# Layer 1 of a two-layer graph network: first row factors moved by 256 bytes, and a group's end turned one row tile at a time

## Chip, cores and metric

The kernel runs on one core of one Trainium2 chip. The metric is the device time of one launch in microseconds (us). Three runs of the kernel before took 2812.17, 2810.19 and 2810.7 us; their median, 2810.7 us, is what the changed kernel is held against.

## The reference, cut to what matters

Two layers over 4096 nodes with 512 features, each with a LayerNorm and a ReLU ahead of it and a residual behind it. The change touches layer 1 only, which is an attention over all nodes with 8 heads of 64 columns:

```
data1 = (h @ W.T + b).reshape(N, H, D)
src = einsum('nhd,xhd->nh', data1, src_proj); trg = einsum('nhd,xhd->nh', data1, trg_proj)
e = src.T[:, :, None] + trg.T[:, None, :]
e = where(e >= 0, e, 0.01 * e) + adj
out = einsum('hnm,hmd->hnd', softmax(e), data1)
x = x + out
```

The kernel writes exp(leaky(src + trg) + adj) as a product of a row factor (z, one per head and destination node), column factors (g_m and d_m, one per head and source node) and exp(adj). So a tile of the scores is one `max` and one multiplication by exp(adj).

## The kernel before, in words

**Groups and steps.** Layer 1 runs over 8 groups: 4 blocks of 1024 destination nodes (WL) times 2 sets of 4 heads (HG). A group has 32 steps (NT), one for each tile of 128 source nodes, m = 0 to 31. In every step VectorE (DVE) makes the score tiles `pr` of the four heads (L1168 and L1171, 128x1024 each; in every fourth step, `BY_LOG`, ScalarE makes that of head 0), and TensorE (PE) multiplies them with the values (`values`, L1205) and with a column of factors for the softmax's denominators (`den`, L1210).

**How TensorE is filled.** The value matmuls have 32 columns of weights each, so four of them stand side by side in the array, in column groups 0 to 3 of 32 columns. `cols` in `gather` is the order in which a step addresses the four. A step gives each column group five matmuls: four of L1205 and one of L1210. In the seven steps of `BY_HALF` (4, 8, 12, 16, 20, 24, 28) one more matmul is given to one column group, number n, and the order turns by one afterwards: n is 0, 1, 2, 3, 0, 1, 2 in these seven steps. The last step gives nine more, to the column groups 0, 1, 2, 3, 1, 2, 3 and, at its end, 0 and 1.

**The end of a group.** ScalarE (ACT) copies the four results out of PSUM (`os`, and `od` for the denominators), and the rest is done during the next group, by `finish`: in its step 1 eight small matmuls sort the denominators (L1262), in step 2 VectorE takes their reciprocals (L1266). Then eight row tiles of 128 nodes are to be turned: `turn` (L1278) transposes two 128x128 pieces for each, on the whole array, into `pt`; ScalarE scales them (L1307, four activations for a tile) into `o`; a GpSimd DMA adds the residual x1 to `o` (taken from the list `due` in every fourth step); a SyncE DMA stores `o`. `finish` is a generator that is advanced in the steps listed in `PARTS`: row tiles are turned in pairs, one pair in each of the steps 2, 6, 10 and 14, after that step's matmuls, and the two tiles of a pair are scaled in the two parts that follow. The last group has its own ending, `finish_last`, which is not changed.

**The order of the work.** All of it is written out by hand (`manual_schedule`): each engine's queue holds its instructions in the order of the program. The loop at the end goes through `stages` (load 4 steps ahead, exp(adj) 1 ahead, weighing 1 ahead, ScalarE's factors 2 ahead, and so on, `gather` last) and then advances the ending.

**The start of layer 1.** The loads of the first row factors z (L1364, four DMAs on SyncE's queue, head 3 first) stand behind the load of the first adjacency tile. They need memory. The tiles of layer 1 lie in memory that layer 0 gave back; the pools `mid` and `l1` begin at the same address. Behind that address, per partition, `mid` takes 5,248 bytes, and he_t[0], he_t[1] and he_t[2] take 8,192 each, so he_t[2] ends at 29,824. In layer 1 the l1 tiles take 4,384, six `pr` tiles 24,576, and the pool s0 608 (pick 32, gap 64, zt0 512), so that z of head 3 begins at 29,568: 256 bytes within he_t[2]. That one holds the layer's bias and projection rows (L862) until the last product at L889. Then come `row_factors` (L1373 on VectorE, L1374 on ScalarE), the column factors g_m and d_m, the first step's four products, and `ngd_m` (L1394), which ScalarE's first `relus` (L1140) needs.

Of the kernel before, what the change touches and what calls it, by code (L numbers as in the profile page):

```python
# [8 lines left out]
FP = mybir.dt.float32  # L9
AF = mybir.ActivationFunctionType  # L10
ALU = mybir.AluOpType
# [4 lines left out]
P = 128  # L16
# [12 lines left out]
def kernel(  # L29
# [15 lines left out]
    nc = tc.nc  # L45
    N, F = x.shape
    H, D = 8, 64
    HG, WL = 4, 1024
    WT = WL // P
    NT = N // P  # L50
# [12 lines left out]
    x1 = dram.tile([N, F], FP, name="x1")  # L63
# [39 lines left out]
    with tc.tile_pool(name="w0", bufs=1) as wp, tc.tile_pool(name="a0", bufs=2) as ap_, tc.tile_pool(  # L103
        name="a0s", bufs=8
# [75 lines left out]
        def turn(t):  # L180
            b, j = divmod(t, TB)
            if j == 0:
                hts[b] = ap_.tile([P, KC, BL], FP, name="h_t")
            if t >= T0:
                nc.vector.transpose(
                    hts[b][:, :, j * P:(j + 1) * P].rearrange("p k (a q) -> p k a q", q=S),
                    hqs.pop(t).rearrange("p (a k q) -> p k a q", k=KC, q=S))
                return
            h = hs.pop(t)
            pt = pp.tile([P, KC, P], FP, name="bank")  # L190
            for k in range(KC):
                nc.tensor.transpose(pt[:, k, :], h[:, k * P:(k + 1) * P], ident)
            nc.vector.tensor_copy(hts[b][:, :, j * P:(j + 1) * P], pt)
            logit(t, h)
# [291 lines left out]
    with tc.tile_pool(name="mx0", bufs=1) as mx0, tc.tile_pool(name="b_b", bufs=3) as adj0, tc.tile_pool(  # L486
        name="mx1", bufs=1
    ) as mx1, tc.tile_pool(name="b_a", bufs=3) as adj1, tc.tile_pool(name="b_m", bufs=4) as mkp, tc.tile_pool(name="b_s", bufs=2) as sp, tc.tile_pool(
        name="b_p", bufs=6, space=PSUM
# [94 lines left out]
        for n in range(-5, len(items)):  # L584
# [3 lines left out]
            if n >= 0:  # L588
                i, j, t = items[n]
# [10 lines left out]
                if n in more:  # L600
                    f, m = more[n]
# [7 lines left out]
    with tc.tile_pool(name="c_x", bufs=1) as ldx, tc.tile_pool(name="c_y", bufs=1) as ldy, tc.tile_pool(  # L609
        name="c_d", bufs=2  # L610
    ) as wkp, tc.tile_pool(name="c_m", bufs=1) as mxp, tc.tile_pool(name="c_o", bufs=4) as iop, tc.tile_pool(
        name="c_s", bufs=2
    ) as sp, tc.tile_pool(name="c_q", bufs=1, space=PSUM) as p_q, tc.tile_pool(
        name="c_p", bufs=1, space=PSUM
# [12 lines left out]
        steps = [(n, q) for n in range(NB) for q in mixed(n)]  # L627
# [121 lines left out]
        left, scale, norms, zs = [], {}, iter(()), {}  # L749
# [25 lines left out]
        def denominators(n):  # L775
            b = ORDER_B[n]
            sc = sp.tile([P, TB], FP, name="sc")
            nc.vector.tensor_tensor(sc, zs.pop(n), dr[:, b * TB:(b + 1) * TB], ALU.add)
            nc.vector.reciprocal(sc, sc)
            nc.vector.tensor_tensor(sc, sc, na[:, b * TB:(b + 1) * TB], ALU.mult)  # L780
            scale[n] = sc
# [3 lines left out]
        def finish(n, j):  # L785

            b = ORDER_B[n]
            oc = iop.tile([P, F], FP, name="xt")
            blk[n][1].append(oc)
            for c, half in enumerate((2, 3) if j < 2 else (4, 5)):  # L790
                nc.scalar.activation(oc[:, c * F2:(c + 1) * F2], cs_[half][:, (j % 2) * F2:(j % 2 + 1) * F2], AF.Copy,
                                     scale=scale[n][:, j:j + 1])
            nc.gpsimd.dma_start(oc, xb_d[rows_of(b * TB + j), :], accum_op=ALU.add)
# [168 lines left out]
        pt = bank(7)  # L962
# [17 lines left out]
    g_m = l1.tile([P, H, NT], FP, name="g_m")  # L980
    d_m = l1.tile([P, H, NT], FP, name="d_m")
    ngd_m = l1.tile([P, H // HG, NT], FP, name="ngd_m")
# [27 lines left out]

    PARTS = (0, 1, 2, 4, 5, 6, 8, 9, 10, 12, 13, 14, 16, 17, 18, 22)
    BY_LOG = (3, 7, 11, 15, 19, 23, 27, 31)
    BY_HALF = (4, 8, 12, 16, 20, 24, 28)
    BY_DMA = [m for m in range(NT - 1) if m not in BY_HALF]
# [2 lines left out]
    with tc.tile_pool(name="p", bufs=2) as prp, tc.tile_pool(name="s0", bufs=1) as s0, tc.tile_pool(  # L1019
        name="za", bufs=1  # L1020
    ) as zp0, tc.tile_pool(name="e", bufs=4) as ep, tc.tile_pool(name="p0", bufs=3) as pr0p, tc.tile_pool(name="rl", bufs=2) as rlp, tc.tile_pool(
        name="io1", bufs=2
    ) as iop, tc.tile_pool(name="s1", bufs=1) as sp, tc.tile_pool(name="e3", bufs=2) as e3p, tc.tile_pool(
        name="zb", bufs=1
    ) as zp1, tc.tile_pool(name="ac", bufs=2) as acp, tc.tile_pool(
        name="os", bufs=1
    ) as osp, tc.tile_pool(name="u", bufs=1) as usp, tc.tile_pool(
        name="p_x", bufs=1, space=PSUM
# [35 lines left out]


        pick = s0.tile([P, 2, 4], FP, name="pick")
        s0.tile([P, 16], FP, name="gap")
        row = ident.rearrange("p (r s) -> p s r", s=Q)
        nc.vector.tensor_copy(pick, row[:, 0:2, :])
        nc.vector.tensor_tensor(pick[:, 1, 0:HV], pick[:, 1, 0:HV], row[:, 2, HV:2 * HV], ALU.add)  # L1070
# [52 lines left out]
        def early_logs(i, m):  # L1123
            logs(i, m, True)
# [15 lines left out]
            nc.scalar.activation(r, zs_[i, 0], AF.Relu, bias=ngd_m[:, h // HG, m:m + 1], scale=d_m[:, h, m:m + 1])  # L1140
            rl[i, m] = r

        due = []

        def sums(i, m):
            if m < 2:
# [5 lines left out]
        def weigh(i, m, order=ORDER):  # L1152
            if m % 4 == 1 and due:
                due.pop()()
            if m:
                sums(i, m - 1)
            h = groups[i][1] * HG
            x_ = ex.pop((i, m))
            for k in order:
                if (i, m, k) in pr:  # L1160
                    continue
                w = (prp if k else pr0p).tile([P, WL], FP, name=f"pr{k}")
                if k == 0 and (i, m) == (0, 0):
                    r = rlp.tile([P, WL], FP, name="rl")
                    nc.vector.tensor_scalar(r, zs_[0, 0], g_m[:, 0, 0:1], d_m[:, 0, 0:1], ALU.max, ALU.mult)
                    nc.vector.tensor_tensor(w, r, x_, ALU.mult)
                elif k == 0:
                    nc.vector.scalar_tensor_tensor(w, rl.pop((i, m)), ngd_m[:, h // HG, m:m + 1], x_,  # L1168
                                                   op0=ALU.subtract, op1=ALU.mult)
                else:  # L1170
                    p_ = nc.vector.scalar_tensor_tensor(w, zs_[i, k], g_m[:, h + k, m:m + 1],  # L1171
                                                        e3.pop((i, m)) if k == 3 else x_,
                                                        op0=ALU.max, op1=ALU.mult)
                    if k == 3:
                        add_logs(i, m + 1, 1, p_)
                pr[i, m, k] = w
            w = pr[i, m, 3]
            if m == 1:
                acc[i, 3] = acp.tile([P, WL], FP, name="acc3", bufs=1)
                nc.gpsimd.tensor_tensor(acc[i, 3], pr[i, 0, 3], w, ALU.add)  # L1180
            elif m > 1:
                nc.gpsimd.tensor_tensor(acc[i, 3], acc[i, 3], w, ALU.add)  # L1182
            add_logs(i, m + 2, 0)
            if m == BY_HALF[0]:
                acc[i, 0, 2] = acp.tile([P, BL], FP, name="acc02", bufs=1)
                nc.gpsimd.tensor_copy(acc[i, 0, 2], pr[i, m, 0][:, BL:])
            elif m in BY_HALF:
                nc.gpsimd.tensor_tensor(acc[i, 0, 2], acc[i, 0, 2], pr[i, m, 0][:, BL:], ALU.add)
# [80 lines left out]
        def share(rd, t, r):  # L1269
            q, j = divmod(t, JT)  # L1270
            k = ORDER[r]
            e, r4 = (0, (k - 1) * HV + q) if k in (1, 2) else (1, (HV if k else 0) + q)
            return rd[:, j, e, r4:r4 + 1]
# [7 lines left out]
        def part(ap, i, t, n):  # L1281

            b, g = groups[i]
            t += b * WT
            return ap[t * P:(t + n) * P, g * HG * D:(g + 1) * HG * D].rearrange("(j p) (h d) -> p j h d", p=P, h=HG)

        def finish(i):


            dens = denominators(i)  # L1290
            os_ = next(dens)
            yield
            next(dens)
            yield
            rd = next(dens)
            old = []
            for t in range(0, WT, 2):
                pt = p_t.tile([P, 2, HG, D], FP, name="pt")
                for j in range(2):
                    turn(os_, t + j, pt[:, j, :, :])  # L1300
                if t > 2:
                    nc.sync.dma_start(part(out, i, t - 4, 2), old.pop(0))
                yield
                o = iop.tile([P, 2, HG, D], FP, name="o")
                for j in range(2):
                    for r, k in enumerate(ORDER):
                        nc.scalar.activation(o[:, j, k, :], pt[:, j, r, :], AF.Copy, scale=share(rd, t + j, r))  # L1307
                    if j == 0:
                        yield
                old.append(o)  # L1310
                due.append(lambda o=o, t=t: nc.gpsimd.dma_start(o, part(x1, i, t, 2), accum_op=ALU.add))
                yield
            nc.sync.dma_start(part(out, i, WT - 4, 2), old.pop(0))
            yield
            nc.sync.dma_start(part(out, i, WT - 2, 2), old.pop(0))
            yield

        def finish_last(i):

# [71 lines left out]
            nc.gpsimd.tensor_copy(d0_m[:, 2 * g:2 * g + 2, :, 0], d_m[:, HG * g + 1:HG * g + 3, :])  # L1391
        nc.gpsimd.tensor_copy(d0_0[:, :, 0], d0_m[:, :, 0, 0])  # L1392
        weigh(0, 0, (3, 1, 2, 0))
        nc.vector.scalar_tensor_tensor(ngd_m, g_m[:, 0::HG, :], -1.0, d_m[:, 0::HG, :], op0=ALU.mult, op1=ALU.mult)  # L1394
        factors(0, 1)
        early_logs(0, 3)
        scale(0, 1)

        stages = ((load, 4), (exps, 1), (rest, 0), (weigh, 1), (factors, 2), (logs, 4), (early_logs, 5), (scale, 2), (gather, 0))
        for s in range(len(steps)):  # L1400
            for f, ahead in stages:
                if s + ahead < len(steps):
                    f(*steps[s + ahead])
            if s == 0:
                ending = iter(())
            elif s == 2:
                ending = tables()
            elif s % NT == 0:
                ending = finish(s // NT - 1)
            if s == len(steps) - 2:  # L1410
                ending = finish_last(len(groups) - 1)
            if s < NT or s % NT in PARTS or s > len(steps) - 3:
                next(ending, None)
        for _ in ending:
            pass

# [33 lines left out]
```

## Time and profile before

| what | us |
|---|---|
| median of three runs | 2810.7 |
| the profiled execution: its time | 2813.82 |
| its span, first to last instruction | 2812.0 |
| TensorE busy, over the span | 2756.2 (98%) |
| VectorE busy | 2506.3 (89%) |
| ScalarE busy | 1476.8 (53%) |
| GpSimd busy | 1464.4 (52%) |
| first matmul of layer 1 | at 1613.34 |
| first matmul of the denominators' sorting (L1262) in the ends of groups 0, 2 and 3 | at 1778.6, 2073.52 and 2220.82 |

The profiled execution took 1.82 us more than its span, and 3.1 us more than the median of the runs. A row of the timeline has the start, the duration, the engine, the line, the operation, the tiles, the shape and how many instructions are joined in it. Idle time of an engine that isn't the bottleneck costs nothing, and a matmul's duration (0.59 us) is longer than the distance to the next on the same columns, because matmuls are pipelined.

### The profile page before, as it was taken

What the parts mean: (1) busy time and instruction counts of PE and PEld (TensorE: products, weight loads), DVE (VectorE), ACT (ScalarE), POOL (GpSimd) and SP (SyncE); (2) the same over time, 40 slices, a digit from 0 to 9 for tenths busy, and PEclk for the clock granted to TensorE, in tenths of its full rate; (3) what the DMA queues carried; (4) which work ended last, traced back from release to release, by engine and by line L of the source; (5) the groups of instructions that cost most, each with busy time, mean ns of one, the idle gap of its engine ahead of it and who ended that gap; (6) DMA issues with size and microseconds to landing.
All of it is one profiled execution on the core that took longest, in us unless ns stands there. A gap on an engine that the chain in (4) does not pass through costs nothing.

```text
span 2812.0 us, 46753 instructions
## 1 busy us (share of the span) xinstructions
PE 2756.2 (98%) x16747; PEld 1495.8 (53%) x16747; DVE 2506.3 (89%) x3427; ACT 1476.8 (53%) x2218; POOL 1464.4 (52%) x1234
## 2 busy tenths in 40 slices
PE   7999999998999999999999799999999999999998
PEld 4885444444888888888885323323232323232322
DVE  7877799898888888888886799999999999999998
ACT  2212232333123333433432188998888888888786
POOL 5323344444011010111106688897979797979886
PEclk9999999999999999999999999999999999999999
DMA  5536898888889999999966379999999999989897
GB/s 174 176 103 252 275 333 300 304 295 262 196 206 197 197 259 203 228 256 209 232 194 169 109 183 242 240 224 242 225 241 231 240 227 237 223 244 225 217 218 172
DMA packets 535992, 629.85 MB, mean 224 GB/s; under 512 B 292152, under 2 KB 346456, under 8 KB 535760
## 3 DMA queue, kind: packets, MB, share of 16 engines
q1 hardware_dynamic: 461920, 415.87, 49.4%
q0 software_dynamic: 71824, 207.07, 34.0%
q10 hardware_dynamic: 2016, 3.93, 0.4%
q8 instruction: 131, 2.15, 0.3%
q14 instruction: 101, 0.83, 0.1%
HBM read 404.23 MB, written 107.15 MB: 182 GB/s over the span
## 4 chain that ended last, share of the span: by engine, by line
PE 84%; DVE 6%; issue 3%; DMA 3%; SPq 2%; ACT 1%; POOL 1%; DVEq 0%; POOLq 0%; ACTq 0%
PE pv L1205 29%; PE po L744 24%; PE pe L531 12%; PE dn L1210 9%; PE bank L267 6%; PE po L878 4%; DVE pr L1171 2%; SPq L671 1%; DMA et<-er_d 1%; DVE mk L520 1%; PE pt L1278 1%; DMA xt<-in_x_dram 1%; ACT e L1114 0%; DVE pr L1168 0%; PE bank L200 0%
## 5 line engine op out<-in xcount | busy, mean ns | idle before, releaser
L1205 PE MATMUL pv<-pr,sup 128*32 128x512 f32 x8192 | 1053.0, 594 | 13.4 <-POOL d L1392 9.4
L1171 DVE SCALAR_TENSOR_TENSOR pr<-z,g_m,ex 128x1024 f32<-128x1024 f32 x512 | 630.6, 1271 | 6.0 <-PE dn L1210 5.6
L1205 PEld LDWEIGHTS pv<-pr,sup 128*32 128x32 f32 x8192 | 304.2, 110 | 611.5 <-issue 563.3
L1182 POOL TENSOR_TENSOR acc<-acc,pr 128x1024 f32<-128x1024 f32 x240 | 576.4, 2402 | 99.5 <-DVE pr L1171 95.8
L531 PE MATMUL pe<-he_t,he_t 128*128 128x512 f32 x896 | 388.2, 594 | 0.0
L1210 PE MATMUL dn<-pr,d_m 128*2 128x512 f32 x1984 | 385.8, 592 | 0.0
L705 ACT ACTIVATE d<-d 128x1024 f32<-128x1024 f32 x126 | 133.2, 1057 | 435.8 <-DVE d L697 231.2
L1104 ACT ACTIVATE ex<-e 128x1024 f32<-128x1024 f32 x256 | 263.3, 1028 | 157.8 <-DVE pr L1171 156.6
L1171 DVE SCALAR_TENSOR_TENSOR pr<-z,g_m,e 128x1024 f32<-128x1024 f32 x256 | 345.9, 1351 | 0.3
L1114 ACT ACTIVATE e<-e,ld_m 128x1024 f32<-128x1024 f32 x256 | 291.5, 1139 | 0.0
L531 PEld LDWEIGHTS pe<-he_t,he_t 128*128 128x128 f32 x896 | 169.8, 191 | 209.5 <-issue 194.7
L744 PE MATMUL po<-he_t,at 128*128 128x256 f32 x1024 | 263.9, 380 | 4.2 <-ACT he_t L755 3.4
L744 PE MATMUL po<-sup,u 128*128 128x256 f32 x1024 | 263.3, 379 | 0.0
L1168 DVE SCALAR_TENSOR_TENSOR pr<-rl,ngd_m,ex 128x1024 f32<-128x1024 f32 x191 | 242.8, 1271 | 5.4 <-ACT ex L1104 4.8
L744 PE MATMUL po<-sup,at 128*128 128x256 f32 x1024 | 242.8, 380 | 1.9 <-DVE mc L537 1.0
L1140 ACT ACTIVATE rl<-z,ngd_m,d_m 128x1024 f32<-128x1024 f32 x191 | 235.0, 1231 | 1.7 <-DVE ngd_m L1394 1.7
L831 POOL DMA_DIRECT2D he_t<-he_t x56 | 48.9, 951 | 352.3 <-ACT he_t L747 301.9
L715 DVE TENSOR_TENSOR at<-d,a 128x1024 f32<-128x1024 f32 x126 | 154.2, 1224 | 78.3 <-PE po L744 41.0
L744 PEld LDWEIGHTS po<-he_t,at 128*128 128x128 f32 x1024 | 194.9, 191 | 31.5 <-issue 3.8
L744 PEld LDWEIGHTS po<-sup,at 128*128 128x128 f32 x1024 | 194.9, 191 | 29.5 <-DVE at L715 1.7
L744 PEld LDWEIGHTS po<-sup,u 128*128 128x128 f32 x1024 | 193.9, 190 | 26.0
L536 POOL DMA_DIRECT2D er_d<-mk x136 | 74.7, 550 | 235.3 <-DVE rm L533 223.5
(272 smaller groups left out, 3927.8 us busy)
## 6 DMA issues: line engine op xcount, KB each, us to landing
e<-in_adj_t_dram SPq DMA_DIRECT2D x256, 512.0 KB, 6.1
acc<-pr POOLq DMA_DIRECT2D x192, 512.0 KB, 6.3
a<-in_adj_t_dram SPq DMA_DIRECT2D x126, 512.0 KB, 5.1
ac<-in_adj_t_dram SPq DMA_DIRECT2D x124, 256.0 KB, 5.2
ar<-in_adj_dram SPq DMA_DIRECT2D x120, 256.0 KB, 4.8
ec_d<-mc POOLq DMA_DIRECT2D x120, 256.0 KB, 5.0
er_d<-mk POOLq DMA_DIRECT2D x112, 256.0 KB, 4.8
et<-er_d SPq DMA_DIRECT2D x448, 64.0 KB, 4.0
```

Source lines behind the costliest of these rows:

```text
L267: nc.tensor.matmul(acc[:, j, :], w, m, start=(k == 0), stop=(k == KC // 2 - 1))
L531: nc.tensor.matmul(pe[:, :w], he_t[i][:, k, (t % TB) * P:(t % TB + 1) * P], he_t[j][:, k, BL - w:], start=(k == 0), stop=(k == KC - 1))
L715: nc.vector.tensor_tensor(w, d, aj.pop((n, q)), ALU.mult)
L744: nc.tensor.matmul(acc[:, j, :], A[:, j * P:(j + 1) * P], B, start=(first_ and j == 0), stop=last, skip_group_check=True)
L1104: nc.scalar.activation(x_, ra.pop((i, m)), AF.Exp)
L1114: nc.scalar.activation(x_, ra[i, m], AF.Exp, bias=ld_m[:, h // HG, m:m + 1])
L1140: nc.scalar.activation(r, zs_[i, 0], AF.Relu, bias=ngd_m[:, h // HG, m:m + 1], scale=d_m[:, h, m:m + 1])
L1168: nc.vector.scalar_tensor_tensor(w, rl.pop((i, m)), ngd_m[:, h // HG, m:m + 1], x_, op0=ALU.subtract, op1=ALU.mult)
L1171: p_ = nc.vector.scalar_tensor_tensor(w, zs_[i, k], g_m[:, h + k, m:m + 1], e3.pop((i, m)) if k == 3 else x_, op0=ALU.max, op1=ALU.mult)
L1182: nc.gpsimd.tensor_tensor(acc[i, 3], acc[i, 3], w, ALU.add)
L1205: nc.tensor.matmul(v[c][q][col * Q:(col + 1) * Q, :], va[:, m, g * HG + k, c0:c0 + Q], pr[i, m, k][:, q * BL:(q + 1) * BL], start=(m == 0) ...
L1210: nc.tensor.matmul(dn[col * Q:col * Q + w.shape[1], :], w, src, **fl)
```

## The change

Four edits, all in layer 1.

1. The unused tile `gap` has 80 floats in place of 16: the z tiles of even groups, and what lies behind them, start 256 bytes further on.
2. `ngd_m` is computed in `weigh`, between the first step's products of head 3 and head 1, and no longer after all four.
3. ScalarE's first `lg` (for step 3) stands behind the exp(adj) of step 1, and no longer ahead of it.
4. `finish` is no generator any more. It is called in every step with the step's number m; a row tile is turned in each of the eight steps of `TURNS` (for the last but one group's end, `LAST_TURNS`), scaled in the step behind it, and every second tile stored later, in a step that is a multiple of four, the last pair of a group at step 32, which is step 0 of the group after next.

```diff
-    PARTS = (0, 1, 2, 4, 5, 6, 8, 9, 10, 12, 13, 14, 16, 17, 18, 22)
+    TURNS = (3, 5, 9, 12, 16, 19, 23, 25)
+    LAST_TURNS = (3, 5, 9, 11, 15, 17, 21, 22)
...
-        s0.tile([P, 16], FP, name="gap")
+        s0.tile([P, 80], FP, name="gap")
...
+                if (i, m, k) == (0, 0, 1):
+                    nc.vector.scalar_tensor_tensor(ngd_m, g_m[:, 0::HG, :], -1.0, d_m[:, 0::HG, :],
+                                                   op0=ALU.mult, op1=ALU.mult)
...
-        def finish(i):
...
+        def finish(i, m):
+
+            if m == 1:
+                got[i] = denominators(i)
+                turned[i] = next(got[i])
+                next(got[i])
+            if m == 2:
+                got[i] = next(got[i])
+            at = TURNS if i < len(groups) - 2 else LAST_TURNS
+            for t in range(WT):
+                j = t % 2
+                if j and m == ((at[t] + 1) // 4 + 2) * 4:
+                    nc.sync.dma_start(part(out, i, t - 1, 2), turned.pop((i, t - 1))[1])
+                if m == at[t]:
+                    if j == 0:
+                        turned[i, t] = p_t.tile([P, 2, HG, D], FP, name="pt"), iop.tile([P, 2, HG, D], FP, name="o")
+                    turn(turned[i], t, turned[i, t - j][0][:, j, :, :])
+                if m == at[t] + 1:
+                    pt, o = turned[i, t - j]
                     for r, k in enumerate(ORDER):
-                        nc.scalar.activation(o[:, j, k, :], pt[:, j, r, :], AF.Copy, scale=share(rd, t + j, r))
...
+                        nc.scalar.activation(o[:, j, k, :], pt[:, j, r, :], AF.Copy, scale=share(got[i], t, r))
+                    if j:
+                        due.append(lambda o=o, t=t: nc.gpsimd.dma_start(o, part(x1, i, t - 1, 2), accum_op=ALU.add))
...
-        nc.vector.scalar_tensor_tensor(ngd_m, g_m[:, 0::HG, :], -1.0, d_m[:, 0::HG, :], op0=ALU.mult, op1=ALU.mult)
         factors(0, 1)
-        early_logs(0, 3)
         scale(0, 1)
...
+            if s == 0 and f is exps:
+                early_logs(0, BY_LOG[0])
...
-            elif s % NT == 0:
-                ending = finish(s // NT - 1)
+            for i in range(max(s // NT - 2, 0), s // NT):
+                finish(i, s - (i + 1) * NT)
...
-            if s < NT or s % NT in PARTS or s > len(steps) - 3:
-                next(ending, None)
+            next(ending, None)
```

More of the change, by code (lines that the diff above doesn't have):

```diff
@@ L1141, in relus @@
             rl[i, m] = r
-        due = []
+        due, got, turned = [], {}, {}
         def sums(i, m):
@@ L1285, in part @@
             return ap[t * P:(t + n) * P, g * HG * D:(g + 1) * HG * D].rearrange("(j p) (h d) -> p j h d", p=P, h=HG)
-        def finish(i):
[L1290 to L1305, printed above, removed]
-                    for r, k in enumerate(ORDER):
-                        nc.scalar.activation(o[:, j, k, :], pt[:, j, r, :], AF.Copy, scale=share(rd, t + j, r))
[L1308 to L1316, printed above, removed]
```

## The prediction

> **What bounds it.** I read the page's busy times first:
>
> ```profile
> PE 2756.2 (98%) x16747; PEld 1495.8 (53%) x16747; DVE 2506.3 (89%) x3427; ACT 1476.8 (53%) x2218; POOL 1464.4 (52%) x1234
> ```
>
> Two engines are near full, so the shares don't say which one ends last where. The table of stages does, cut at the groups of layer 1 (here group 0 and one of the later ones). Columns: the stretch, its length, then busy us (and instructions) of PE, PE's weight loads, DVE, ACT, POOL; the granted clock, the DMA share, GB/s.
>
> ```profile
> 1613.00:1764.00 151.00, 145.65 (x1270) 48.99 (x1274) 148.84 (x123) 127.83 (x170) 131.00 (x93) 0.98 0.82 213
> ...
> 2064.00:2211.30 147.30, 147.30 (x1343) 44.57 (x1339) 145.80 (x122) 120.65 (x142) 125.46 (x82) 1.00 0.93 235
> ```
>
> In group 0 PE has gaps and DVE has hardly any: DVE sets the pace there. In groups 2 to 7 (the others' rows are alike) PE has no gap at all, while DVE, 1.5 us below the length, has a few. So two parts of the change meet two different limits: an earlier start is kept through group 0, and what is added to PE's queue in the later groups is paid in full.
>
> Next, what PE's 147.30 us are made of, from its timeline. A step of nothing special takes 4.29 us (1788.91 to 1793.20 below): ten slots of 0.429. A matmul takes two slots of its column group, 0.86; call that a unit. A turned pair in step 2:
>
> ```profile
> 1784.00 0.66 PE L1278 MATMUL pt<-ident,os 128*128 128x128 f32 x4
> ...
> 1784.59 3.64 PE L1205 MATMUL pv<-pr,sup 128*32 128x512 f32 x32
> ...
> 1788.91 3.62 PE L1205 MATMUL pv<-pr,sup 128*32 128x512 f32 x32
> ```
>
> Step 2 began at 1779.57 and takes 5.02, step 3 takes 4.32, so the pair costs 0.70. Now step 4, which has a `BY_HALF` matmul (first two rows), and the pair in step 6:
>
> ```profile
> 1793.20 0.59 PE L1210 MATMUL dn<-pr,zo 128*2 128x512 f32 x1
> 1793.20 0.61 PE L1205 MATMUL pv<-pr,sup 128*32 128x512 f32 x3
> ```
>
> ```profile
> 1801.36 1.44 PE L1210 MATMUL dn<-pr,d_m 128*2 128x512 f32 x5
> 1802.73 0.66 PE L1278 MATMUL pt<-ident,os 128*128 128x128 f32 x4
> 1803.32 0.64 PE L1205 MATMUL pv<-pr,sup 128*32 128x512 f32 x4
> ```
>
> The extra matmul costs step 4 nothing: column group 0 works on it while the other three begin the next step (1793.20: one `dn`, three `pv`), and from then on it is a unit behind. But a transposition needs the whole array. At 1801.36 three column groups finish their step; column group 0 has two slots still to go, and the transposes begin 1.37 us after that row (in step 2, with no lag: 0.54, from its last `dn` at 1783.46). Step 6, 1797.50 to 1803.32, takes 5.82, a unit less 0.06 above step 2 with its pair. So **a turn costs 0.70, and a unit more if a column group lags**. If there is no turn between, four `BY_HALF` matmuls lag four different column groups and cost one unit together.
>
> Check on a whole group: 32 x 4.293 = 137.39; sorting (L1262) 1.12; four pairs 2.81; drains in steps 6, 10 and 14, 3 x 0.859 = 2.58; the `BY_HALF` steps 16 to 28, one unit, 0.86; step 31's nine matmuls give column group 1 three units, 2.58. Sum 147.34; measured 147.30 (the sorting's matmuls start at 2073.52 and 2220.82). PE's own queue explains the group with nothing left for waits.
>
> **Edit 4, the turns.** Four transposes stand about 0.11 us apart within their 0.66, so one tile costs 0.70 less 2 x 0.11 = 0.485, an estimate from that row; eight cost 3.88 where four pairs cost 2.81: +1.07. Drains: the turns of steps 5, 9, 12, 16, 23 and 25 each follow a `BY_HALF` step (4, 8, 12, 16, 20, 24) with no turn between, those of 3 and 19 don't: six units, 5.15, where there were 3 + 1, 3.43: +1.72. Step 28 then lags column group 2 alone. Step 31 gives that one two units and column group 1 three, so 2.58 as before, if the lag is taken up there. New group: 137.39 + 1.12 + 3.88 + 5.15 + 2.58 = 150.12, **+2.79**. The last group, by `LAST_TURNS`: drains in 5, 9, 15, 17 and 21; steps 24 and 28 lag column groups 1 and 2, and step 31 ends four units late in column group 1: again 150.1.
>
> Is the lag taken up in step 31? The order there is column groups 3, 0, 1, 2, and 3 is busy with a late `dn`:
>
> ```profile
> 2060.54 0.59 PE L1210 MATMUL dn<-pr,zo 128*3 128x512 f32 x1
> 2060.55 0.62 PE L1205 MATMUL pv<-pr,sup 128*32 128x512 f32 x1
> 2060.55 0.59 PE L1210 MATMUL dn<-acc,zo 128*2 128x512 f32 x1
> 2060.56 1.00 PE L1210 MATMUL dn<-pr,zo 128*3 128x512 f32 x2
> ```
>
> One `pv` starts beside three `dn`, in column group 0, though one for column group 3 is ahead of it in the queue. A blocked column group doesn't hold the others there, so I take "taken up"; in strict order each of groups 1 to 6 would lose a unit more (+5.2 in all), which I keep for the range. The Trainium skill, "TensorE: Matmul & The Clock Gate", Architectural detail: the array is 16× 32×32, says of PE's queue that it is a partial reorder window which pulls weight loads ahead of running matmuls; of matmuls passing one another it says nothing, and read strictly it would add that 5.2. Here the row decides.
>
> A second rule of the skill speaks against the edit: "TensorEngine Tiling (Array Packing)", Tiling Modes, Key Properties, has it that a change of the tiling mode drains TensorE, while a change of tile does not. Taken alone, without the lag, it would charge only four more switches a group, 7 x 1.07 = 7.5 us, and with the start below the sum would be 2812.8; the row at 1801.36 adds the lag that is drained.
>
> The rest of the edit lies beside this. ACT's 32 scalings per group stay 32 (ACT is busy 120.65 of 147.30); accumulating DMAs and stores stay four; SyncE's queue gains, since a store now comes four steps behind its accumulating DMA instead of two, with the adjacency loads behind it four steps ahead. DVE, with 145.80 to do in 150.1, is late for nothing new. No new wait enters PE's queue: `pt` is read one step after each turn and the next pair comes two or more steps later.
>
> **Edits 1 to 3, the start.** SyncE's own waits show one entry for the z loads:
>
> ```profile
> SPq L1364 <- DVE a L889: 33.6, 1, 33.6
> ```
>
> From 1567.6 the loads stand ready and wait for he_t[2]'s last readers, L889. With z 256 bytes further on they begin where he_t[2] ends, so they go at about 1567.6 instead of 1602.28. What is late then is tmb (VectorE, 1603.99) and four small copies behind it, to about 1604.75.
>
> ```profile
> 1606.66 0.76 DVE L1373 TENSOR_SCALAR z<-z,tmb 128x1024 f32<-128x1024 f32 x1 [1.85 <-DMA z<-s_d]
> ...
> 1620.96 1.28 DVE L1168 SCALAR_TENSOR_TENSOR pr<-rl,ngd_m,ex 128x1024 f32<-128x1024 f32 x1 [2.13 <-ACT ex L1104]
> ```
>
> ```profile
> 1617.73 1.24 ACT L1140 ACTIVATE rl<-z,ngd_m,d_m 128x1024 f32<-128x1024 f32 x1 [1.69 <-DVE ngd_m L1394]
> 1618.88 1.13 ACT L1120 ACTIVATE lg<-u,nlg_m 128x1024 f32<-128x1024 f32 x1
> 1619.91 1.01 ACT L1104 ACTIVATE ex<-e 128x1024 f32<-128x1024 f32 x1
> ```
>
> The first z goes 1.9 earlier; ACT's chain up to the last z (eight activations, whose starts lie 0.96, 0.30, 1.04, 0.41, 0.96, 0.96 and 1.16 apart where nothing is waited for) runs without the wait of 0.54 before 1611.82 too, so that its end, 1615.00, becomes 1612.5, and the first head-0 product, at 1615.44, 1612.6: 2.8 won. It ends at about 1614.65. Before, ACT did three things after that product: rl (behind ngd_m), lg, ex, 1617.73 to 1620.92. Now rl is done by 1614.7, lg stands behind, and only ex (1.01) is left: DVE's 1620.96 becomes 1615.85. **5.1 won** in all. It is carried through group 0, as DVE paces it. What could change it are the steps 4 to 6, where DVE's product of head 3 takes 2.79, 1.60 and 2.46 instead of 1.28 beside POOL's work: between 3 and 8.
>
> **Sum.** Start -5.1; group 1 +2.79 less 0.3, which it lost to DVE (1778.6 to 2073.52 is two groups, 294.92, where two of 147.30 make 294.60); groups 2 to 7, 6 x 2.79 = 16.74. Total **+14.1**. The profiled execution's 2813.82 becomes 2827.9; it lies 3.1 above the median of the runs, so the runs should show 2810.7 + 14.1 = **2824.8**.
>
> **Rivals.**
> - *Strict order in step 31*: +5.2 more, 2830.0. For it: program order. Against: the `pv` row at 2060.55. Chance 0.14.
> - *Faster: one tile slips through.* If two transposes no longer drain the lag (in PE's place between two steps, price 0.86 each), the three drains of before go as well, PE falls to about 145.9 and DVE's 145.80, with its waits some 146.8, becomes the bound: -0.5 x 7 and the start's -5.1 give 2802.1. It decides from the point where a group's PE work is under 146.8. For it: two transposes are half of four. Against: the wait at 1801.36 comes before the first one. Chance 0.07.
> - *No change*: a single tile costs half a pair after all (0.35), and one of the two added drains hides in weight loads: 7 x 0.86 = 6.0, less the start's 5.1 and group 1's 0.3, is 2811.3. For it: the weight loads at L1278 overlap. Against: 0.27 of a pair's 0.70 is there whatever its number of transposes. Chance 0.07.
> - *The loads don't move* (another old tile lies there too): of the 5.1 only the 2.2 of edits 2 and 3 stay, 2827.7. For it: layer 0's buffers overlap these tiles nearly everywhere. Against: the semaphore names L889, and with it he_t[2], alone. Chance 0.07, within the range.
>
> **Numbers.** Forecast 0.65 and the two slower rivals 0.21: slower 0.86; same 0.07; faster 0.07. 0.2% (5.6 us) is about what a measurement of this kernel can tell from no change. Range: with a single tile at 0.40 (56 turns, -4.8) and a start of 8 the low end is 2817; with strict order, a tile at 0.53 and a start of 3 the high end is 2835. I take 2815 to 2836, which leaves out the faster case and part of "no change".
>
> **What would show it.** In the changed profile: steps 5, 9, 12, 16, 23 and 25 of a group 5.6 long on PE, steps 3 and 19 about 4.8; 150.1 between the sortings of two groups; z loads issued before 1570, the second step's head-0 product near 1616, group 1's sorting near 1773.5. Wrong if groups stay at 147, or if DVE or ACT shows waits that PE doesn't cause.

## The result, and the profile after

The changed kernel took 2826.14 us (median of six runs, 2822.55 to 2828.61) beside 2810.49 for the kernel before (six runs, 2806.81 to 2812.59): a ratio of 1.0054, 95% interval 1.0044 to 1.0064, so +15.65 us. The forecast was 2824.8. The mechanism is the one that was forecast; of what the start of layer 1 wins, 0.8 us less was left at the end of group 0 than the forecast had. Lines below L1010 have moved: the values' matmuls are L1209 now (were L1205), the denominators' L1214 (L1210), the turn L1282 (L1278), the head products L1172 and L1175 (L1168 and L1171), GpSimd's scaling L1099 (L1098), its adds of the fourth head and its half adds L1186 and L1192 (L1182 and L1188), the z loads L1361 (L1364).

**The page's busy times** moved on TensorE above all, by 19.4 us (VectorE's by 5.0, the others' by less):

```profile
PE 2775.6 (98%) x16747; PEld 1496.6 (53%) x16747; DVE 2511.3 (89%) x3427; ACT 1474.5 (52%) x2218; POOL 1463.0 (52%) x1234
```

The same instructions in number, but more time on PE, and no gap: where the transposes wait, the late column group is still at work (the rows of step 5 below), and PE counts as busy.

**The table of stages**, cut at group 0, group 1 and one later group (columns as in the prediction):

```profile
1609.00:1764.40 155.40, 150.13 (x1318) 51.18 (x1320) 154.47 (x125) 132.77 (x175) 136.20 (x101) 0.96 0.83 213
1764.40:1914.60 150.20, 150.20 (x1340) 43.67 (x1337) 147.85 (x123) 134.29 (x201) 127.33 (x84) 1.00 0.92 231
2064.70:2214.80 150.10, 150.10 (x1341) 44.19 (x1337) 146.45 (x122) 120.40 (x142) 125.41 (x83) 1.00 0.92 230
```

From group 1 on PE has no gap, as before, but the length is 150.1 where it was 147.30, and DVE now has 3.7 us to spare. From sorting to sorting the groups take 150.11, 150.11 and four times 150.12 (before: 147.64, then 147.30 five times), and the last stretch, to the sorting of `finish_last`, 142.46 (139.64).

**Steps on PE.** Step 3, which has no lag, began at 2079.54 and ends at the last row's start:

```profile
2082.97 1.04 PE L1214 MATMUL dn<-pr,d_m 128*2 128x512 f32 x8
2083.95 0.44 PE L1282 MATMUL pt<-ident,os 128*128 128x128 f32 x2
2084.31 3.64 PE L1209 MATMUL pv<-pr,sup 128*32 128x512 f32 x32
```

4.77, so two transposes cost 0.48. Step 5, behind the `BY_HALF` step 4, began at 2088.64:

```profile
2092.49 0.59 PE L1209 MATMUL pv<-pr,sup 128*32 128x512 f32 x1
2092.50 1.44 PE L1214 MATMUL dn<-pr,d_m 128*2 128x512 f32 x5
2093.87 0.44 PE L1282 MATMUL pt<-ident,os 128*128 128x128 f32 x2
2094.24 1.06 PE L1209 MATMUL pv<-pr,sup 128*32 128x512 f32 x8
```

The transposes start 1.37 behind the `dn` row instead of 0.54 behind the last `dn`: the late column group is waited for. The step takes 5.61, that is 0.84 above step 3, and so do 9, 12, 16, 23 and 25; step 19 takes 4.77, and step 31 6.03, as before. In step 31, with column group 2 a unit behind since step 28, PE's timeline of the same group has:

```profile
2210.51 0.60 PE L1214 MATMUL dn<-acc,zo 128*2 128x512 f32 x3
2210.93 0.59 PE L1209 MATMUL pv<-pr,sup 128*32 128x512 f32 x1
2210.94 1.01 PE L1214 MATMUL dn<-acc,zo 128*2 128x512 f32 x4
```

Three of the step's nine extra `dn` begin while one column group is still at its values. The late one is column group 2, so the three are those of 0, 1 and 3; in the program column group 2's stands ahead of 3's.

**The start.** The z loads leave SyncE early, and their wait for L889 is gone; what is left is this one, for layer 0's store of s_d (lines from SyncE's waits and, below, from its timeline):

```profile
SPq L1361 <- DMA s_d<-a: 2.4, 1, 2.4
```

```profile
1531.10 0.32 SPq L1361 DMA_DIRECT2D z<-s_d  x1
...
1539.56 1.40 SPq L1361 DMA_DIRECT2D z<-s_d  x3
```

Layer 0 ends a few us earlier or later in each execution, so from here on the start is measured from tmb, VectorE's copy at the end of layer 0 (L969): 1603.99 before, 1603.76 after. (With an unchanged start, the kernel before, e2 and e6 below differ by up to 0.7 us at step 1 and 0.6 at group 1, so a difference of two executions is no better than that.) From there the first z comes at +0.73 (before +2.66), step 1's head-0 product at +11.46 (+16.96), step 8's head-3 product at +45.69 (+49.88), group 1's first matmul at +160.61 (+164.94), and the span's end at +1223.07 (+1208.05). So 5.5 us are won at step 1, 4.3 of them are left at group 1, and from there to the end 19.35 are lost: 2.47 in group 1, 14.1 in groups 2 to 6 (2.81 or 2.82 each), 2.82 in the last stretch. Together +15.0.

### The profile page after: what moved, and what is told of

It reads as the page before. It is cut to its first block, busy times and chain, and to the rows that moved or that the text cites. A ratio compares the mean times of both kernels' runs of the same rounds, so it can differ in the third digit from the quotient of the medians.

```text
span 2826.8 us, 46754 instructions
## 1 busy us (share of the span) xinstructions
PE 2775.6 (98%) x16747; PEld 1496.6 (53%) x16747; DVE 2511.3 (89%) x3427; ACT 1474.5 (52%) x2218; POOL 1463.0 (52%) x1234
## 3 DMA queue, kind: packets, MB, share of 16 engines
q8 instruction: 131, 2.15, 0.3%
## 5 line engine op out<-in xcount | busy, mean ns | idle before, releaser
L1209 PE MATMUL pv<-pr,sup 128*32 128x512 f32 x8192 | 1021.4, 595 | 9.6 <-DVE ngd_m L1164 5.5
L1175 DVE SCALAR_TENSOR_TENSOR pr<-z,g_m,ex 128x1024 f32<-128x1024 f32 x512 | 630.8, 1272 | 15.5 <-PE dn L1214 11.5
L1186 POOL TENSOR_TENSOR acc<-acc,pr 128x1024 f32<-128x1024 f32 x240 | 576.2, 2401 | 117.3 <-DVE pr L1175 112.4
L1209 PEld LDWEIGHTS pv<-pr,sup 128*32 128x32 f32 x8192 | 294.1, 110 | 592.3 <-issue 541.5
L1175 DVE SCALAR_TENSOR_TENSOR pr<-z,g_m,e 128x1024 f32<-128x1024 f32 x256 | 349.5, 1365 | 2.4 <-DVE rd L1270 1.3
L1214 PE MATMUL dn<-pr,d_m 128*2 128x512 f32 x1984 | 340.5, 592 | 0.0
L1172 DVE SCALAR_TENSOR_TENSOR pr<-rl,ngd_m,ex 128x1024 f32<-128x1024 f32 x191 | 242.8, 1271 | 7.3 <-ACT ex L1105 7.1
```

The source lines that it names most:

```text
L1209: nc.tensor.matmul(v[c][q][col * Q:(col + 1) * Q, :], va[:, m, g * HG + k, c0:c0 + Q], pr[i, m, k][:, q * BL:(q + 1) * BL], start=(m == 0) ...
L1214: nc.tensor.matmul(dn[col * Q:col * Q + w.shape[1], :], w, src, **fl)
```

## Experiments

**My theory** is the prediction's: a turn of one tile costs PE 0.48, and 0.86 more where a column group lags; what the start wins is carried through group 0; there is nothing else. **Three rivals**: PE's loss comes from the number of turns (eight for four) and not from drained lags; the new addresses of the tiles matter beyond the loads; VectorE or GpSimd slows the later groups. Each experiment is compared with runs of the kernel before on the same chip (2810.71, 2810.23 or 2810.50 us).

### The halves: e1_start_only and e2_turns_only

e1 is the kernel before with edits 1 to 3 (`ngd_m` and `early_logs` moved as in the change):

```diff
-        s0.tile([P, 16], FP, name="gap")
+        s0.tile([P, 80], FP, name="gap")
...
+                if (i, m, k) == (0, 0, 1):
+                    nc.vector.scalar_tensor_tensor(ngd_m, g_m[:, 0::HG, :], -1.0, d_m[:, 0::HG, :],
...
-        early_logs(0, 3)
```

e2 is the kernel before with edit 4 alone (`finish` and its calls as in the change):

```diff
-    PARTS = (0, 1, 2, 4, 5, 6, 8, 9, 10, 12, 13, 14, 16, 17, 18, 22)
+    TURNS = (3, 5, 9, 12, 16, 19, 23, 25)
+    LAST_TURNS = (3, 5, 9, 11, 15, 17, 21, 22)
...
-        def finish(i):
+        def finish(i, m):
```

> Edits 1 to 3 alone (gap, ngd_m, the first lg); the row tiles are turned in pairs as before. My theory: the start's gain is independent of the turns and is carried through group 0, as in the changed kernel's trace, where group 1 begins 4.6 us earlier (1764.37 for 1768.93): the later groups stay at 147.3 us, and the time is 4.6 below the kernel before, about 2805.9. Rival (the gain is eaten in group 1, where the pairs meet a VectorE that is no further ahead): group 1 grows by what was won, 2810.

> Edit 4 alone: one row tile at a time by TURNS and LAST_TURNS, the start as in the kernel before. My theory: groups of 150.12 us, so 7 x 2.8 less the 0.3 that group 1 lost to VectorE: +19.3, about 2829.8. Rival (part of the groups' growth comes from the other start, by a phase that is carried on): less than +17, under 2827.

e1 took 2807.09, ratio 0.9987 (0.9978 to 0.9996); e2 2829.07, ratio 1.0068 (1.0054 to 1.0082). From tmb to the end e1 gains 4.3 us and e2 loses 18.8; together +14.5, near the +15.0 of both. A later group of each, by the table of stages:

```profile
2056.20:2203.50 147.30, 147.30 (x1344) 44.60 (x1342) 146.13 (x122) 120.61 (x142) 125.51 (x82) 1.00 0.93 235
```

```profile
2064.80:2215.00 150.20, 150.20 (x1344) 44.23 (x1341) 146.31 (x122) 120.51 (x142) 125.52 (x83) 1.00 0.93 230
```

With the new addresses and the old turns a group keeps its 147.30; with the old addresses and the new turns it takes 150.1. In the later groups the addresses matter for nothing, and the loss belongs to edit 4. VectorE has nothing to do with it: its busy time is within 0.2 in the two, and beside PE's 150.2 it has 3.9 to spare.

### Which part of the start: e5_gap_only, e6_gap_64, e7_order_only

e5 and e6 change the kernel before in the size of `gap` alone, to 80 floats in e5 and to 64 in e6; e7 has edits 2 and 3 alone, and `gap` stays at 16. The diff of e6:

```diff
-        s0.tile([P, 16], FP, name="gap")
+        s0.tile([P, 64], FP, name="gap")
```

> Edit 1 alone: gap of 80 floats, all else as before. My theory (memory shared with he_t[2] held the z loads): they are issued before 1550 us, the first z is worked on 0.7 us after tmb where it was 2.7, and the first head-0 product of step 1 comes about 2.9 us earlier seen from tmb (16.96 becomes 14.1); ngd_m and lg still stand before ex. Carried to group 1 that is about -2.9, 2807.8, less what the steps beside GpSimd's scaling take back. Rival (the address itself makes the products faster): VectorE's products of groups 2, 4 and 6 get shorter than 1.27 us.

> As the kernel before, with a gap of 64 floats: the z tiles move by 192 bytes, so 64 bytes still lie within he_t[2]. My theory: the loads wait as before (issued at about 1602, 33 us of waiting), the time is unchanged. Rival (any other address helps, or alignment does): earlier loads or other durations, 2808 or less.

> Edits 2 and 3 alone: ngd_m between the first step's products, the first lg behind exp(adj) of step 1; z loads as late as before. My theory: rl is done when the first step's products end and only ex (1.0 us) is left before the first head-0 product of step 1, which comes 2.2 us earlier seen from tmb (16.96 becomes 14.8); group 1 begins 2.2 earlier at best, 2808.5. Rival (ScalarE is busy with the late z anyway, so that rl has no room before the products end): less than 1.

| kernel | median, ratio (95%) | won at step 1 | won at group 1 |
|---|---|---|---|
| e5, gap 80 | 2807.77, 0.9989 (0.9980 to 0.9999) | 3.16 | 3.16 |
| e6, gap 64 | 2810.52, 0.9998 (0.9989 to 1.0008) | -0.27 | -0.10 |
| e7, order | 2809.50, 0.9997 (0.9988 to 1.0007) | 2.53 | 1.30 |
| e1, both | 2807.09, 0.9987 (0.9978 to 0.9996) | 5.52 | 4.27 |

The last two columns are from the profiled executions, both counted from tmb; by the runs alone e7 can't be told from no change. The rival of e5, that the address itself makes VectorE faster, falls: in groups 2, 4 and 6 its products take 1.27 us in the mean for heads 0 to 2 and 1.33 to 1.34 for head 3, in e5 as in the kernel before. With 64 floats, 64 bytes short of he_t[2]'s end, the z loads go at 1600.7 and SyncE's wait is back to the same 33.6:

```profile
SPq L1364 <- DVE a L889: 33.6, 1, 33.6
```

So it is the overlap of addresses and nothing gradual. And e5 keeps all it wins, while e7 loses half: what is given back belongs to the new order of edits 2 and 3. Within one execution it is plainer: from step 1's head-0 product to group 1's first matmul it takes 147.8 to 148.0 in the four kernels without these edits (before, e2, e5, e6), and 149.2 in e7, e1 and the changed kernel. It goes in step 3. VectorE's and GpSimd's timelines there, first of the kernel before, then of the changed one:

```profile
1629.31 1.32 DVE L1171 SCALAR_TENSOR_TENSOR pr<-z,g_m,e 128x1024 f32<-128x1024 f32 x1
```

```profile
1627.15 2.39 POOL L1182 TENSOR_TENSOR acc<-acc,pr 128x1024 f32<-128x1024 f32 x1
```

```profile
1623.59 2.71 DVE L1175 SCALAR_TENSOR_TENSOR pr<-z,g_m,e 128x1024 f32<-128x1024 f32 x1
```

```profile
1622.66 2.39 POOL L1186 TENSOR_TENSOR acc<-acc,pr 128x1024 f32<-128x1024 f32 x1
1625.05 1.90 POOL L1099 TENSOR_SCALAR sup<-sup,d_m 128x64 f32<-128x64 f32 x2
```

Before, the product took 1.32 (so it does in e5; in e7 it takes 2.71), and it began (1629.31) only when GpSimd's add was all but done (1627.15 + 2.39 = 1629.54). Now it begins 0.93 into the add and ends 1.25 after it, at 1626.30: as long as if it had waited for the add and then taken its usual 1.3. The scaling behind it, two instructions that take 0.85 together when alone, begins while the product still runs and takes 1.90: it seems to have waited in its turn. The four products of a step differ in this: head 3's reads both z and e from SBUF, where those of heads 1 and 2 read `ex` from PSUM; and they, in the same stretch of the trace, keep their 2.46 for two. By step 8 all of the loss is there: 34.23 from step 1's head-0 product to step 8's head-3 product, where it was 32.92.

### Fewer drains: e3_singles_few_drains

Against the changed kernel:

```diff
-    TURNS = (3, 5, 9, 12, 16, 19, 23, 25)
-    LAST_TURNS = (3, 5, 9, 11, 15, 17, 21, 22)
+    TURNS = (2, 3, 6, 7, 10, 11, 14, 15)
+    LAST_TURNS = (2, 3, 6, 7, 10, 11, 14, 15)
```

> The changed kernel with both lists of turns at 2, 3, 6, 7, 10, 11, 14, 15: eight single tiles, but only three of the turns follow a BY_HALF step. My theory (a drain of a lagging column group costs 0.86, a single tile 0.485): groups of 137.39 + 1.12 + 3.88 + 4 x 0.859 + 2.58 = 148.40, 1.72 less than in the changed kernel; 12.0 us below it, about +2.9 on the kernel before, 2813.4. Rival A (it is the number of separate turns that costs, each with its own drain): 150.1 as in the changed kernel, 2826. Rival B (ScalarE's scalings come late and hold up exp(adj)): slower than the changed kernel, because four of the eight scalings now fall into the steps 3, 7, 11 and 15, where ScalarE also makes lg: over 2826.

It took 2874.73, ratio 1.0224 (1.0210 to 1.0238): a badly made test. The turns themselves cost what the theory says, 4.80 us for steps 2, 3 and 7, and 5.61 for 6, 10 and 14, but steps 11 and 15 take 5.8 to 9.4. ScalarE's and PE's waits in one group:

```profile
ACT o L1311 <- DMA out_dram<-o: 7.3, 2, 3.7
```

```profile
PEld pt L1282 <- ACT o L1311: 7.1, 2, 3.8
```

There are two `o` buffers. A tile pair's store is issued in a step that is a multiple of four, and with this list ScalarE wants the buffer one step earlier; PE, in order, waits for ScalarE to empty `pt`. The time is over 2826, as rival B forecast, and ScalarE's scalings do come late, but for the buffers and not for `lg`. On drains as against turns the time says nothing.

### Turns as many, drains fewer: e10_turns_shifted

Against the changed kernel:

```diff
-    TURNS = (3, 5, 9, 12, 16, 19, 23, 25)
+    TURNS = (3, 5, 7, 12, 13, 15, 24, 25)
```

> The changed kernel with TURNS = (3, 5, 7, 12, 13, 15, 24, 25), LAST_TURNS as they are: still eight single tiles, four stores, a similar spread and no scaling in a step with lg, and BY_HALF untouched, so GpSimd's work stays; but only the turns of 5, 12 and 24 find a lag. The stores come in the steps 12, 20, 24 and 32, before their buffers are written again. My theory: groups 1 to 6 take 147.5 on TensorE, 2.6 less each than in the changed kernel: 15.5 below it, 2810.6, a little more where VectorE (147.1) interferes. Rival (eight separate turns cost their drains): 150.1 per group, 2826. Rival (something else than TensorE binds these groups, as ScalarE's waits for buffers did with turns in 2, 3, 6 and 7): over 2820.

Eight single turns, three of them (5, 12, 24) behind an undrained lag. It took 2814.56, ratio 1.0013 (1.0003 to 1.0022). A later group:

```profile
2059.70:2207.50 147.80, 147.65 (x1340) 44.95 (x1336) 145.67 (x122) 120.24 (x142) 125.36 (x82) 1.00 0.93 234
```

Steps 5, 12 and 24 take 5.61, steps 3, 7 and 15 4.77. With the same number of turns a group is 2.3 us shorter than the changed kernel's: the three drains less do that, and the rival that puts the whole loss on the number of turns falls. (By the prediction's sum the number of turns has a share, 1.07 of the 2.79 a group; the drains have 1.72.) The 0.3 over the expected 147.5 stand in steps 13 (4.80) and 25 (5.0, in group 1 6.27), whose turn follows another in the step before, and waits until ScalarE has scaled that one out of the `pt` bank (PE's timeline in group 1):

```profile
1883.99 0.44 PE L1282 MATMUL pt<-ident,os 128*128 128x128 f32 x2 [1.41 <-ACT o L1311]
```

Group 1 takes 149.65, 2.15 over the 147.5, and the five groups behind it 0.3 each: 3.8 of the 4.0 us by which the time lies above the 2810.6 that were expected.

### The extra matmuls moved instead: e8_halves_moved

Against the changed kernel:

```diff
-    BY_HALF = (4, 8, 12, 16, 20, 24, 28)
+    BY_HALF = (7, 8, 11, 12, 20, 23, 28)
```

> The changed kernel with its turns untouched, but BY_HALF at 7, 8, 11, 12, 20, 23 and 28 in place of every fourth step: now only the turns of 9, 12 and 23 (in the last group 9, 11, 15 and 21) find a lag. My theory: groups 1 to 6 take 137.39 + 1.12 + 3.88 + 3 x 0.859 + 2.58 = 147.5, the last 0.9 less than in the changed kernel: 6 x 2.6 + 0.9 = 16.4 below it, about 2809.7. The turns of 5, 16 and 25 take a step of 4.78, where they took 5.61. Rival (eight separate turns cost their drains wherever the extra matmuls stand): 150.1 per group, 2826. Rival (the adds on GpSimd that go with these steps come late): VectorE or ScalarE waits appear, over 2815.

The steps did as the theory says: 5, 16 and 25, which no lag precedes now, take 4.77; 9, 12 and 23 5.61. The kernel did not: 2826.52, ratio 1.0052 (1.0037 to 1.0068). VectorE, 148.32 of 149.10 busy, has become the bound:

```profile
2067.40:2216.50 149.10, 148.87 (x1345) 43.89 (x1342) 148.32 (x122) 120.06 (x141) 128.75 (x82) 1.00 0.92 231
```

In a `BY_HALF` step GpSimd makes a half add (L1192) behind its add (L1186); moved, these meet other products. VectorE's and GpSimd's timelines at step 13 show where one meets a product:

```profile
2117.84 1.32 DVE L1175 SCALAR_TENSOR_TENSOR pr<-z,g_m,e 128x1024 f32<-128x1024 f32 x1
2122.90 2.10 DVE L1175 SCALAR_TENSOR_TENSOR pr<-z,g_m,e 128x1024 f32<-128x1024 f32 x1
```

```profile
2118.05 2.27 POOL L1192 TENSOR_TENSOR acc<-acc,pr 128x512 f32<-128x512 f32 x1
...
2122.63 1.28 POOL L1192 TENSOR_TENSOR acc<-acc,pr 128x512 f32<-128x512 f32 x1
```

At 2117.84 the product is first and the half add takes 2.27; at 2122.63 the half add is first and the product takes 2.10, ending 1.09 after it. Group 0 is 2.7 longer than the changed kernel's as well. That the time is the one that the rival of the turns forecast is chance: of the six steps of 5.61 a group three have gone. Here the third rival, VectorE and GpSimd, is right, but only here: in the changed kernel VectorE has its 3.7 us to spare in every later group.

### Pairs with other steps: e4_pairs_late, e9_pairs_late_scale_act

e4 turns pairs, two of the four with a lag before them (steps 6 and 16). e9 also gives ScalarE the scaling that GpSimd did in group 0's steps 3 to 5.

Both against the changed kernel, with the store in step `(SCALES[t] // 4 + 2) * 4`:

```diff
-    TURNS = (3, 5, 9, 12, 16, 19, 23, 25)
-    LAST_TURNS = (3, 5, 9, 11, 15, 17, 21, 22)
+    TURNS = (2, 2, 6, 6, 16, 16, 19, 19)
+    SCALES = (4, 5, 8, 9, 17, 18, 20, 21)
...
-                if m == at[t] + 1:
+                if m == SCALES[t]:
```

In e9 besides:

```diff
-                    if m < (6, 3)[i]:
+                    if m < (3, 3)[i]:
```

> The changed kernel with pairs again, turned in the steps 2, 6, 16 and 19 and scaled in 4, 5, 8, 9, 17, 18, 20 and 21. By step 16 the steps 8, 12 and 16 have lagged three different column groups, so one drain pays for three, and step 19 has no lag. My theory: TensorE's work per group is 137.39 + 1.12 + 2.81 + 2 x 0.859 + 4 x 0.859 = 146.47 (the steps 20, 24 and 28 add one unit at the end), under VectorE's 146.8, which then is the bound: 0.5 less per group than before and the start's 4.6: about 2802.2. Rival A (the number of turns counts, not where they stand): as with the start alone, 2805.9. Rival B (later turns and stores cost): over 2806.

> As the kernel with pairs turned in 2, 6, 16 and 19, and besides the scaling of the values of group 0 in the steps 3, 4 and 5 is moved from GpSimd (L1099) to ScalarE. My theory: VectorE's products of head 3 in group 0's steps 3, 4 and 6 take 2.7, 2.7 and 2.5 us instead of 1.3 because GpSimd's two small L1099 stand beside them; without these, group 0 is up to 4 us shorter, 2801.5. Rival (it is GpSimd's accumulating adds, or ScalarE becomes late by the two activations of 0.58 us per step): 2805 or more.

e4 took 2805.61, ratio 0.9981 (0.9972 to 0.9990); e9 2802.52, ratio 0.9973 (0.9962 to 0.9984), the fastest of all. A later group of e4, and a wait of PE's within it:

```profile
2057.30:2204.50 147.20, 147.20 (x1344) 47.68 (x1339) 146.09 (x122) 120.45 (x141) 125.41 (x82) 1.00 0.94 234
```

```profile
PEld pv L1209 <- DVE pr L1175: 3.6, 11, 0.9
```

The median, 2805.61, is what rival A forecast by the number of turns, but the steps are those of the theory: 5.83 for step 16 with three lags drained at once, 4.99 for step 19 with none. Without the waits PE would need 146.47 by the sum; its steps 26, 29 and 30 take 4.58, 4.74 and 4.88 where 4.29 is due. These are 1.3 together, and the group is 0.7 over the sum; that late column groups catch up in the waits is argued, not shown. So VectorE, 146.09 busy, holds these groups at 147.1 to 147.2, not at 146.8, and one drain less than the kernel before buys 0.15 a group and not 0.86.

In e9 GpSimd's adds of steps 3 to 5 are no longer held up behind the scaling, and the products of steps 4, 5 and 6, where e4 has 2.72, 1.60 and 2.45, take 1.32, 1.27 and 1.28. VectorE's row of step 4:

```profile
1626.92 1.32 DVE L1175 SCALAR_TENSOR_TENSOR pr<-z,g_m,e 128x1024 f32<-128x1024 f32 x1
```

Group 0 is 2.6 us shorter than e4's (group 1's first matmul at +158.08 from tmb, e4 +160.72). Step 3's product still takes 2.56, beside the add at 1621.12. So the scaling is not itself what the products meet there, as the expectation had it: without it the adds come early enough in steps 4 to 6, and in step 3 it is the add alone, as the rival had it.

## Why the prediction was right, and where it was off

1. *What bounds it.* Right. The later groups take what PE takes, before and after; group 0 takes what VectorE takes (154.47 of 155.40 busy).
2. *A single tile 0.485, a drain 0.859.* Measured 0.48 and 0.84, in the changed kernel and again in e2, e8 and e10. That a drain is charged for the lag and not for the turn is shown by e10 and e8: moving either the turns or the extra matmuls moves the 0.84.
3. *A new group 150.12, and 150.1 by `LAST_TURNS`.* Measured 150.11 to 150.12, and +2.82 for the last stretch.
4. *The lag of step 28 is taken up in step 31.* Right: step 31 takes 6.03, as before, and no group takes 150.98. The rival of strict order is refuted. The prediction said that the Trainium skill is silent on matmuls that pass one another. The section that it named is, but Part 2 of the same page, "TensorE: Matmul & The Clock Gate", says "The MATMULs themselves stay in program order", which is the rival's side. The 150.12 us of groups 1 to 6, the changed kernel's row at 2210.51, and the kernel before's at 2060.55, speak against that for matmuls of different column groups; the measurement decides.
5. *The z loads go at about 1567.6.* Wrong in the time: 1531.10 and 1539.56. The prediction took their place in SyncE's queue as fixed, behind layer 0's last fetches (L867, done at 1567.5 in the kernel before). In the changed kernel they stand among these fetches, still behind the first adjacency load (L1083, at 1512.84), and the next three adjacency loads went with them, at 1541.48 for 1604.24; e5, with the gap alone, does the same (1525.04), but how the queue comes by its order no run shows. It cost nothing, since tmb was the later condition either way, as the prediction said.
6. *The start wins 2.8 by the loads and 2.2 by the order.* Measured alone 3.16 (e5) and 2.53 (e7); both together 5.52 (e1) for the 5.1.
7. *"It is carried through group 0, as DVE paces it."* This is the step that failed, by 1.2 us: of 5.5 won at step 1, 4.3 are left at group 1. (In the sum only 0.8 is missing, since by luck step 1 had won 0.4 more than forecast.) The prediction had put the risk at steps 4 to 6 and bounded it at 3 to 8, and the loss is inside these bounds; but it stood in step 3, where a product that had just cleared GpSimd's add now begins within it (2.71 for 1.32). The same pace on VectorE didn't mean the same meeting with GpSimd, whose add came only 4.5 us earlier and not 5.7 (each from its own row: 1627.15 to 1622.66, and 1629.31 to 1623.59). In the kernel before, GpSimd stood idle for 1.96 us, waiting for VectorE, ahead of the add to `lg` in front of this one (1625.91); in the changed kernel there is no idle time left there to give up.
8. *Group 1, +2.79 less 0.3.* Measured +2.47.

The sum: forecast -5.1 + 2.49 + 16.74 = +14.1; measured from tmb to the end -4.3 + 2.47 + 16.9 = +15.0 (with rounding). The runs' +15.65 agrees, with an interval of 12.4 to 18.0. Edit 4's part was nearly exact; what the forecast missed is most of a microsecond at the start.

The other rivals: *one tile slips through* is refuted by the rows of step 5, and its bound on VectorE was wrong as well, 147.1 for 146.8 (e4). *No change* needed 0.35 for a tile and a drain that hides; neither is there. *The loads don't move* is what e6 shows with 64 floats; with 80 they move.

On point 7 the Trainium skill, "SBUF — State Buffer", Who interferes with whom, has a rule that I had not used: a VectorE instruction with two inputs from SBUF and a GpSimd instruction that reads SBUF block one another, and which of them started first decides who waits. The four rows of e8 above, both orders within 6 us, agree with it.

## What to carry to other kernels

Where matmuls are packed by columns, count for each whole-array instruction between them what it drains. Most of the time here was made not by the number of such instructions (e10: eight turns, 147.8 a group), but by the number of lags that they cut off before several could run out together (150.1). An earlier start of a stage is worth only what survives its meetings with the other engines: measure the gain at the end of the stage as well as at its first instruction. And a wait of a load can hang on a few bytes of an old tile: 192 bytes more did nothing, 256 took the whole 33.6 us wait away.

## What the runs showed of the hardware

Matmuls of a free column group start ahead of one that stands earlier in the queue for a busy column group; without that, by the prediction's sum, each of groups 1 to 6 would have taken 0.86 more. VectorE's product of two SBUF tiles, 1.28 alone, takes 2.1 to 2.8 in the rows read above, and 3.22 once in e8, when it begins within a GpSimd add, and the add's neighbours stretch the other way (0.85 to 1.9 for two scalings, 1.28 to 2.27 for a half add). That the earlier instruction decides is read from rows of several kernels; e9 supports it, since it took the scaling away and the products of steps 4 to 6 went back to 1.3, but no run shifted one add alone. Left open is whether the gain of the start can be kept whole in step 3: no version moved that one add away from the product.
